# Mixture of experts: the slots of tokens counted in units of 128, with three positions of 128 slots among 32 of 256

## The chip, the cores and the metric

The kernel runs on one core of a Trainium2 chip. The metric is the time on the device in microseconds (us); the lower, the better. The engines of the core work side by side, each through its own list of instructions in order: TensorE (PE: matmuls and, as PEld, the loading of their stationary operand), VectorE (DVE), ScalarE (ACT), GpSimd (POOL) and SyncE (SP, which only issues transfers). Transfers run on 16 DMA engines that all queues share.

## The reference, cut to what matters

Two layers work on 4 images of 1024 tokens with 384 channels. Layer 0 is an attention and a mixture of experts, layer 1 an outlook attention and a feed-forward part. The change is in the experts of layer 0:

```python
scores = einsum('bsd,de->bse', x, gate_w) + gate_b          # 4 experts
probs = softmax(scores)
masked = probs * (probs among the token's two largest)
masked = masked / (sum(masked) + 1e-9)
h = gelu(einsum('bsd,edh->ebsh', x, w1) + b1, approximate=False)   # 384 -> 1536
y = einsum('ebsh,ehd->ebsd', h, w2) + b2                            # 1536 -> 384
out = einsum('bse,ebsd->bsd', masked, y)
```

Only two of the four experts have a weight other than zero for a token. There are 4096 tokens, so 8192 pairs of a token and an expert. How many tokens an expert gets depends on the data, so it is not known when the program is built.

## The kernel before, in words

Everything is float32. Attention runs first, then `experts`, then `rest` (the outlook attention in `outlook`, the feed-forward part in `Kron`).

**Slots and blocks.** Each token has two slots, one in the list of each of its experts. `Router.route` works out the slots of one image and writes for each slot a line of `table` in memory: the number of the token, its mean and its scale. An expert's list is cut into blocks of XB = 256 slots. As the last block of each of the 4 lists can be filled in part, the kernel is built for NXB = 35 blocks (8192 slots and 4 times 255, divided by 256). All 35 are always computed, whatever the data.

**The order of the blocks.** The first NFIRST = 4 blocks must be full with tokens of images 0 to 2, so that they can begin before the last image is routed; `Router.first` (L1369) picks them. `Router.schedule` (L1431) sets the order of the rest when the last image is routed. It counts for every image and expert how many blocks are begun, so that blocks come in the order in which the images complete them. It is VectorE work on arrays with a few numbers per partition. `Router.rows` (L1395) turns the counts into two lists of row numbers, one number per position: `w` for the rows of the weights of its expert, `t` for the rows of `table`. The last part of `schedule` works out `index`, the row of `yg` from which each token later fetches its two results. `schedule` is a generator: the block loop advances it by `next(beside)` once per up matmul group of blocks 0 to 2 (L1613), behind the last projections and the routing of the last image.

**One block** (`experts`, the loop from L1587). `tokens(n)` gathers the lines of the table, `fetch(n)` gathers the tokens into `xb`, one gather of 128 tokens for each of the block's two tiles, and `weights(n)` gathers the expert's weights, `up` (128 rows of 18,480 bytes) and `down` (128 rows of 19,968 bytes). These are indirect transfers of GpSimd. VectorE normalizes the tokens (`norm`), TensorE transposes them (`turn`) and VectorE copies the result into `xbT`. Then come twelve groups of three up matmuls (L1607: 128 rows, 128 columns of weights, 256 tokens), each with a gelu on ScalarE (L1611), and for each tile of 128 tokens twelve down matmuls (L1624, 384 columns). VectorE adds the bias (L1629) and SyncE writes the tile to `yg` in memory (L1630). Each float32 matmul shows as two records, here called passes.

**What is ahead of what.** The buffers `up`, `down`, `xb` and `xbT` exist twice, for even and odd blocks. At the start of block n the loads for block n+1 are issued in program order; `norm(n+1)` follows the up matmuls of block n, and `turn(n+1)` stands in TensorE's list before the last tile's down matmuls of block n. TensorE, VectorE, ScalarE and SyncE keep the order in which the program is written (a manual schedule); GpSimd's order is set by the framework when the program is built. In the outlook stage it is the other way round: SyncE and GpSimd keep the written order, the other three are ordered at build.

**Adding the results.** `add(i)` gathers a tile's two results from `yg`, weights them and adds them to the residual. Inside the experts one tile is added per block, as soon as all blocks that can hold the tokens of its image are done; `Router.complete(b)` (L1484) gives their number: 15, 23, 31 and 35 for images 0 to 3. That makes 19 tiles in the experts. The other 13 are added in the outlook stage, one in each of its steps from step 4 on (L1704).

Of the kernel before, what the change touches and what calls it, by code (L numbers as in the profile page):

```python
# [10 lines left out]
FP = mybir.dt.float32  # L11
# [32 lines left out]
XB = 256  # L44
NXB = (2 * NT * P + NE * (XB - 1)) // XB
NFIRST = 4


class Net:
# [16 lines left out]
    def slots(self, dram):  # L66

        self.table = dram.tile([NE * NT * P, Router.LINE], mybir.dt.int32, name="table")
        self.yg = dram.tile([NXB * XB, C], FP, name="yg")
        self.room = [dram.tile([P * (BAND + 1) * NH], FP, name=f"room_{t}", tag=f"room_{t}") for t in range(NB)]  # L70
# [1132 lines left out]


class Router:

# [9 lines left out]
    def __init__(self, net, pool, keep, psum):  # L1216
# [25 lines left out]
        self.number = const("number", [P, NXB])  # L1242
        count(self.number, [[1, NXB]])
        self.lane = const("lane", [P, 1])
# [3 lines left out]

        self.next = const("next", [P, B + 1, NE])
        nc.gpsimd.memset(self.next, 1.0)  # L1250
# [118 lines left out]
    def first(self):  # L1369

        nc = self.nc
        shape = [P, NE, self.NJ]
        full = self.temp("full", [P, NE])
        nc.vector.tensor_scalar(full, self.upto[:, B - 1, :], -float(XB), None, ALU.add)
        fills = self.temp("gt", shape)
        nc.vector.tensor_tensor(
            fills, full.unsqueeze(2).to_broadcast(shape), self.steps.unsqueeze(1).to_broadcast(shape), ALU.is_ge
        )
        nc.vector.tensor_reduce(full, fills, AX.X, ALU.add)

        self.start = self.pool.tile([P, B + 1, NE], FP, name="rt_start")
        self.begun = self.pool.tile([P, B + 1, NE], FP, name="rt_begun")
        nc.gpsimd.memset(self.begun[:, 0, :], 0.0)
        pre = self.start[:, 0, :]
        nc.gpsimd.memset(pre[:, 0:1], 0.0)
        for e in range(1, NE):
            nc.vector.tensor_tensor(pre[:, e : e + 1], pre[:, e - 1 : e], full[:, e - 1 : e], ALU.add)
        taken = self.begun[:, 1, :]
        nc.vector.tensor_scalar(taken, pre, -1.0, float(NFIRST), ALU.mult, ALU.add)
        nc.vector.tensor_scalar(taken, taken, 0.0, None, ALU.max)  # L1390
        nc.vector.tensor_tensor(taken, taken, full, ALU.min)
        nc.vector.tensor_scalar(pre, pre, float(NFIRST), None, ALU.min)
        self.firsts = self.rows(self.pool, "first", NFIRST, 1)

    def rows(self, pool, name, n, groups):  # L1395
# [6 lines left out]
        own = self.temp(f"own_{name}", [P, NE])  # L1402
        nc.vector.tensor_scalar(own, self.region, 1.0 / XB, None, ALU.mult)
        nc.vector.tensor_tensor(jump, jump, own.unsqueeze(1).to_broadcast([P, groups, NE]), ALU.add)
# [11 lines left out]
        for what, by, last in (  # L1416
            ("w", self.next[:, :groups, :].rearrange("p g e -> p (g e)"), None), ("t", step, NE * self.NJ - 1),
        ):
            nc.vector.tensor_tensor(part, past, by.unsqueeze(1).to_broadcast(shape), ALU.mult)
            row = self.temp(f"row_{what}_{name}", [P, n])  # L1420
            nc.vector.tensor_reduce(row, part, AX.X, ALU.add)
            if last is not None:
                nc.vector.tensor_tensor(row, row, self.number[:, :n], ALU.add)
                nc.vector.tensor_scalar(row, row, float(last), None, ALU.min)
            nc.vector.tensor_scalar(row, row, float(P), self.lane, ALU.mult, ALU.add)
            rows = self.pool.tile([P, n], mybir.dt.int32, name=f"rows_{what}_{name}")
            nc.vector.tensor_copy(rows, row)
            out.append(rows)
        return out

    def schedule(self, pool):  # L1431
# [3 lines left out]
        fills = self.temp("gt", shape)  # L1435
        taken = self.temp("taken", [P, NE])
        nc.vector.tensor_copy(taken, self.begun[:, 1, :])
        begun = self.temp("ends", [P, B + 1, NE])
        nc.vector.tensor_copy(begun[:, 0, :], taken)
        for b in range(B):  # L1440
            nc.vector.tensor_tensor(
                fills, self.upto[:, b + 1, :].unsqueeze(2).to_broadcast(shape),
                self.steps.unsqueeze(1).to_broadcast(shape), ALU.is_gt,
            )
            nc.vector.tensor_reduce(begun[:, b + 1, :], fills, AX.X, ALU.add)
            nc.vector.tensor_tensor(begun[:, b + 1, :], begun[:, b + 1, :], taken, ALU.max)

        nc.vector.tensor_copy(self.begun[:, 1:, :], begun[:, :B, :])
        fresh = self.temp("fresh", [P, B, NE])
        nc.vector.tensor_tensor(fresh, begun[:, 1:, :], begun[:, :B, :], ALU.subtract)  # L1450
        start = self.start[:, 1:, :]
        nc.vector.tensor_reduce(start[:, :, 0:1], begun[:, :B, :], AX.X, ALU.add)
        for e in range(1, NE):
            nc.vector.tensor_tensor(
                start[:, :, e : e + 1], start[:, :, e - 1 : e], fresh[:, :, e - 1 : e], ALU.add
            )
        yield
        self.all = self.rows(pool, "all", NXB, B + 1)
        yield

        groups = [P, B + 1, NE]
        wide = [P, NT, NE]
        region = self.region.unsqueeze(1).to_broadcast(groups)
        edge, base, move = (self.temp(n, groups) for n in ("edge", "bases", "move"))
        nc.vector.scalar_tensor_tensor(edge, self.begun, float(XB), region, ALU.mult, ALU.add)
        nc.vector.scalar_tensor_tensor(base, self.start, float(XB), edge, ALU.mult, ALU.subtract)
        nc.vector.tensor_copy(move[:, 0, :], base[:, 0, :])
        nc.vector.tensor_tensor(move[:, 1:, :], base[:, 1:, :], base[:, :B, :], ALU.subtract)
        row, past = self.wide(pool, "row", wide), self.wide(pool, "past", wide)
        nc.vector.tensor_tensor(row, self.at, move[:, 0:1, :].to_broadcast(wide), ALU.add)  # L1470
        for g in range(1, B + 1):
            nc.vector.tensor_tensor(past, self.at, edge[:, g : g + 1, :].to_broadcast(wide), ALU.is_ge)
# [10 lines left out]
    @staticmethod  # L1483
    def complete(b):  # L1484

        return min(NXB, NFIRST + (2 * NTOK * (b + 1) + NE * (XB - 1)) // XB)

    def gather(self, y, i, n):

        self.nc.gpsimd.indirect_dma_start(  # L1490
            out=y, out_offset=None, in_=self.net.yg[: self.complete(i // NB) * XB, :],
            in_offset=bass.IndirectOffsetOnAxis(ap=self.index[n][:, i : i + 1], axis=0),
        )


def experts(net, router, x1, x2, wup, wdown, beside):
# [10 lines left out]
    with ExitStack() as ctx:  # L1507
# [23 lines left out]
        ids, xbs = {}, {}  # L1531

        def tokens(n):
            t = ids[n] = halves[0].tile([P, TT, router.LINE], I32, name="ids", tag="ids", bufs=6)
            nc.gpsimd.indirect_dma_start(
                out=t.rearrange("p t w -> p (t w)"), out_offset=None,
                in_=net.table.rearrange("(r t) w -> r (t w)", t=TT),
                in_offset=bass.IndirectOffsetOnAxis(ap=rows(n)[1], axis=0),
            )

        def fetch(n):
            xb = xbs[n] = halves[n % 2].tile([P, TT, C], FP, name="xb", tag="xb")
            last = (B - 1 if n < NFIRST else B) * NTOK
            for t in range(TT):
                nc.gpsimd.indirect_dma_start(
# [4 lines left out]
        def norm(n):  # L1550
            xb = xbs[n]
            own = ids.pop(n).bitcast(FP)
            for t in range(TT):
                nc.vector.tensor_scalar(
# [3 lines left out]
        def turn(n):  # L1558
            xb = xbs.pop(n)
            xbT = halves[n % 2].tile([P, KC, XB], FP, name="xbT", tag="xbT")  # L1560
            for t in range(TT):
                ps = router.psum()
# [24 lines left out]
        for n in range(NXB):  # L1587
# [13 lines left out]
            up, down = ws.pop(n)  # L1601
            hs = []
            for f in range(NF):
                ps = ps_h.tile([P, XB], FP, name="ps_h", tag="h")
                for k in range(KC):
                    o = k * HID + f * P
                    nc.tensor.matmul(  # L1607
                        ps, lhsT=up[:, o : o + P], rhs=xbT[:, k, :], start=k == 0, stop=k == KC - 1,
                    )
                h = hp.tile([P, XB], FP, name="h", tag="h")  # L1610
                nc.scalar.activation(h, ps, AF.Gelu, bias=up[:, KC * HID + f : KC * HID + f + 1])  # L1611
# [5 lines left out]
            else:  # L1617
                net.scale(0, added)
            for t in range(TT):
                if t == TT - 1 and n + 1 < NXB:  # L1620
                    xbT = turn(n + 1)
                ps = ps_y.tile([P, C], FP, name="ps_y", tag="y")
                for f in range(NF):
# [6 lines left out]
                nc.sync.dma_start(  # L1630
                    out=net.yg[n * XB : (n + 1) * XB, :].rearrange("(p t) c -> p t c", t=TT)[:, t, :], in_=y
                )
# [606 lines left out]
```

## Time and profile before

| | |
|---|---|
| median of 3 runs | 2905.45 us (2903.23 to 2907.56) |
| the profiled execution | 2905.3 us, of which its span is 2903.6 |
| mean granted clock of TensorE | 0.965 |
| attention, to the first up matmul of the experts | 0 to 1210.6 us |
| experts, blocks 0 to 34 | 1210.6 to 2345.5 us |
| rest | 2345.5 to 2903.6 us |

The page's second part cuts the span into 40 slices and gives the busy share of each engine in tenths:

```
PE   6889998999999987799999999999999999999988
DVE  1377776777778786532010001111111146877642
ACT  3778777787778774212112111211211122122135
POOL 1000000120021004122111122212121101100000
PEclk9989999999999998799999999999999999999998
DMA  5143435222413334445545455555555437644432
```

Slices 17 to 31 are the experts. How to read such lines: in rows of groups, the columns are line, engine, operation, output and inputs by the program's names, shapes and count, then busy time in us and the mean in ns of one, then the engine's idle time before them and what ended it. In rows in order of time the columns are start and duration in us, engine, line, operation, names, shape and count, and in brackets the idle time before and what released the instruction.

### The profile page before, as it was taken

The page shows a single profiled execution, that of the slowest core. Times are in us where ns is not written, and L with a number is a line of the kernel's source. Part 1 is how long each engine was busy: PE and PEld are TensorE (multiplying, and loading weights), DVE is VectorE, ACT ScalarE, POOL GpSimd, SP SyncE. Part 2 cuts the span into 40 slices and gives each one's busy share as a digit, 9 for nine tenths or more (in the row PEclk, how much of TensorE's full clock was granted, in tenths as well). Part 3 has the DMA queues.
Part 4 walks back from the last instruction along what each step waited for, and adds up shares of the span by engine and source line. Part 5 has one row for each costly group of instructions (what it writes and reads, how often), then busy time and mean ns, then how long its engine had stood idle before and what let it go on. Part 6 is the DMA issues. An engine that isn't in the chain of part 4 may idle for free. (4 is left out here: it accounts for less than half of the span.)

```text
span 2903.6 us, 37519 instructions
## 1 busy us (share of the span) xinstructions
PE 2715.6 (94%) x13632; PEld 1453.0 (50%) x13632; DVE 1347.6 (46%) x3714; ACT 1208.3 (42%) x2023; POOL 401.3 (14%) x500
## 2 busy tenths in 40 slices
PE   6889998999999987799999999999999999999988
PEld 3323333333333322367777777777777754444432
DVE  1377776777778786532010001111111146877642
ACT  3778777787778774212112111211211122122135
POOL 1000000120021004122111122212121101100000
PEclk9989999999999998799999999999999999999998
DMA  5143435222413334445545455555555437644432
GB/s 104 32 103 100 100 92 140 66 59 70 109 44 75 80 90 128 130 149 201 190 169 195 168 200 204 200 212 201 214 202 204 162 132 222 193 161 155 145 106 89
DMA packets 216996, 405.97 MB, mean 140 GB/s; under 512 B 83505, under 2 KB 177905, under 8 KB 203745
## 3 DMA queue, kind: packets, MB, share of 16 engines
q1 hardware_dynamic: 185504, 189.20, 22.2%
q0 software_dynamic: 27152, 209.66, 21.1%
q10 hardware_dynamic: 4144, 4.61, 0.5%
q8 instruction: 110, 1.80, 0.3%
q14 instruction: 86, 0.70, 0.1%
HBM read 305.35 MB, written 49.99 MB: 122 GB/s over the span
## 5 line engine op out<-in xcount | busy, mean ns | idle before, releaser
L1611 ACT ACTIVATE h<-ps_h,up 128x256 f32<-128x256 f32 x420 | 199.0, 474 | 916.5 <-PE ps_h L1607 916.4
L1607 PE MATMUL ps_h<-xbT,up 128*128 128x256 f32 x2520 | 553.5, 380 | 2.6 <-ACT h L1611 1.8
L1624 PE MATMUL ps_y<-down,h 128*128 128x384 f32 x1680 | 554.5, 487 | 0.0
L1607 PEld LDWEIGHTS ps_h<-xbT,up 128*128 128x128 f32 x2520 | 479.9, 191 | 77.9 <-ACT h L1611 2.7
L685 DVE CUSTOM_DVE_ANT_0 e<-e,rz,inv 128x1024 f32<-128x1024 f32 x384 | 475.2, 1274 | 51.8 <-DMA rz<-r_row 49.2
L633 ACT ACTIVATE e<-ps_s,ten 128x1024 f32<-128x1024 f32 x384 | 408.1, 1109 | 59.8 <-PE ps_s L623 36.2
L1624 PEld LDWEIGHTS ps_y<-down,h 128*128 128x128 f32 x1680 | 317.3, 191 | 207.0 <-issue 1.2
L1629 DVE TENSOR_TENSOR y<-ps_y,down 128x384 f32<-128x384 f32 x70 | 39.0, 557 | 718.1 <-PE ps_y L1624 718.1
L623 PE MATMUL ps_s<-q,k 32*128 32x512 f32 x1536 | 295.5, 667 | 53.4 <-ACT e L633 31.5
L641 PE MATMUL ps_o<-e,wv 128*32 128x512 f32 x1536 | 226.1, 664 | 40.5 <-DVE wv L692 39.0
L641 PE MATMUL ps_z<-e,rt_ones 128*32 128x512 f32 x1536 | 218.6, 643 | 0.0
L712 POOL DMA_DIRECT2D q<-po x96 | 76.1, 878 | 946.4 <-DMA q<-po 514.6
L369 ACT ACTIVATE below<-tk_left,tk_bound 128x1024 bf16<-128x1024 f32 (+1 forms) x160 | 184.3, 1152 | 52.3 <-DVE tk_bound L375 42.1
L623 PEld LDWEIGHTS ps_s<-q,k 32*128 32x128 f32 x1536 | 92.0, 189 | 192.2 <-ACT e L633 92.0
L1735 PE MATMUL ps_a<-wa,xnT 128*128 128x486 f32 x384 | 167.6, 585 | 8.7 <-DVE attn L1745 7.0
L284 PE MATMUL ps_t<-xnT,wqkv 128*128 128x512 f32 x288 | 137.1, 617 | 2.4 <-ACT xnT L466 1.7
L641 PEld LDWEIGHTS ps_o<-e,wv 128*32 128x32 f32 x1536 | 31.5, 111 | 199.7 <-issue 68.4
L1735 PEld LDWEIGHTS ps_a<-wa,xnT 128*128 128x128 f32 x384 | 71.7, 192 | 93.4 <-issue 85.3
L641 PEld LDWEIGHTS ps_z<-e,rt_ones 128*32 128x32 f32 x1536 | 52.3, 117 | 132.0 <-issue 128.7
L1576 DVE SCALAR_TENSOR_TENSOR x<-yt,weight,x 128x384 f32<-128x384 f32 x38 | 23.5, 619 | 188.3 <-DMA x<-x 187.6
L1837 PE MATMUL ps_y<-band,v 128*32 128x194 f32 (+2 forms) x960 | 102.7, 517 | 8.0 <-DMA band<-room 7.7
L1490 POOL DMA_INDIRECT yt<-yg,index x64 | 65.5, 1024 | 305.9 <-DVE x L1576 142.4
(346 smaller groups left out, 2739.5 us busy)
## 6 DMA issues: line engine op xcount, KB each, us to landing
band<-room SPq DMA_DIRECT2D x32, 1560.0 KB
rz<-r_row SPq DMA_DIRECT2D x48, 512.0 KB
yg<-y SPq DMA_DIRECT2D x70, 192.0 KB
q<-q SPq DMA_DIRECT2D x192, 64.0 KB
k<-k SPq DMA_DIRECT2D x192, 64.0 KB
room<-none SPq DMA_DIRECT2D x64, 192.0 KB
x<-x SPq DMA_DIRECT2D x38, 192.0 KB
o<-in_x_dram SPq DMA_DIRECT2D x33, 192.0 KB
```

The source lines that it names most:

```text
L284: nc.tensor.matmul(ps, lhsT=lhsT(k), rhs=rhs(k), start=k == 0, stop=k == KC - 1)
L369: nc.scalar.activation(junk[:n], left[:n], AF.Sign, bias=bound[:n], accum_out=over[:n])
L623: nc.tensor.matmul(ps[:, half * 512 : half * 512 + 512], lhsT=self.k4[r, u * P : (u + 1) * P], rhs=self.q4[r, :], start=True, stop=True,)
L633: nc.scalar.activation(e, ps, AF.Exp, bias=shift, scale=QK_SCALE)
L641: nc.tensor.matmul(ps[r : r + 32, :], lhsT=lhsT(odd), rhs=self.es[2 * u + odd][:, half * 512 : half * 512 + 512], start=u == 0, stop=u == ...
L685: nc.vector.tensor_tensor_reduce(self.es[m], self.es[m], self.rz, 1.0, self.im["inv"][:, m, self.h : self.h + 1], ALU.mult, ALU.add, self. ...
L712: nc.gpsimd.dma_start(out=there, in_=po[r : r + 32, :], accum_op=ALU.add)
L1607: nc.tensor.matmul(ps, lhsT=up[:, o : o + P], rhs=xbT[:, k, :], start=k == 0, stop=k == KC - 1,)
L1611: nc.scalar.activation(h, ps, AF.Gelu, bias=up[:, KC * HID + f : KC * HID + f + 1])
L1624: nc.tensor.matmul(ps, lhsT=hs[f][:, t * P : (t + 1) * P], rhs=down[:, f * C : (f + 1) * C], start=f == 0, stop=f == NF - 1,)
L1735: nc.tensor.matmul(pa[:, hh, :HW_], lhsT=xnT[:, k, :], rhs=wa[:, k, hh * HW_ : (hh + 1) * HW_], start=k == 0, stop=k == KC - 1,)
L1837: nc.tensor.matmul(ys[c][32 * n : 32 * n + 32, lo - 512 * half : hi - 512 * half], lhsT=vs[b, t][:, h * HD : (h + 1) * HD], rhs=bands[b, t ...
```

## The change

Slots are counted in units of 128. There are NFULL = 32 positions of 256 slots and NHALF = 3 of 128. The order of positions is: four full ones (0 to 3, as before), three of 128 slots (4 to 6), and 28 full ones (7 to 34). `schedule` gives the three short positions to experts whose remaining slots end in the first half of a block of 256; if more than 32 full blocks would otherwise be needed, it gives one to the first 128 slots of such a block. `first_row(n)` is the row of `yg` at which position n begins.

```diff
-NXB = (2 * NT * P + NE * (XB - 1)) // XB
+NFULL = 2 * NT * P // XB
+NHALF = NE - 1
+NXB = NFULL + NHALF
 NFIRST = 4
+NLEAD = NFIRST + NHALF
+UNITS = XB // P
...
+def first_row(n):
+
+    half = min(max(n - NFIRST, 0), NHALF)
+    return (n - half) * XB + half * P
```

`first` scales its two results by UNITS (one more instruction). `rows` works on B + 2 = 6 groups of 4 experts in place of 5, and scales the rows in up to three pieces:

```diff
-            nc.vector.tensor_scalar(row, row, float(P), self.lane, ALU.mult, ALU.add)
+            for first, end in ((0, min(n, NFIRST)), (NFIRST, min(n, NLEAD)), (NLEAD, n)):
+                if first < end:
+                    size = P if last is None or first == NFIRST else P // UNITS
+                    own = row[:, first:end]
+                    nc.vector.tensor_scalar(own, own, float(size), self.lane, ALU.mult, ALU.add)
```

In `schedule` the choice of the short positions comes first, then the counts per image:

```diff
+        part, left, odd, pairs, sums = (self.temp(n, [P, NE]) for n in ("base", "part", "share", "run", "prob"))
+        nc.vector.tensor_scalar(part, self.upto[:, B, :], -float(P), None, ALU.add)
+        blocks(pairs, part)
+        blocks(odd, self.upto[:, B, :])
+        nc.vector.tensor_tensor(odd, odd, pairs, ALU.subtract)
+        ahead(sums, odd)
+        nc.vector.tensor_scalar(sums, sums, NHALF + 0.5, None, ALU.is_lt)
+        nc.vector.tensor_tensor(odd, odd, sums, ALU.mult)
+        nc.vector.scalar_tensor_tensor(left, first, -1.0 / UNITS, pairs, ALU.mult, ALU.add)
+        nc.vector.tensor_scalar(left, left, 0.5, None, ALU.is_gt)
+        ahead(sums, left)
+        nc.vector.tensor_scalar(sums, sums, 1.5, float(UNITS), ALU.is_lt, ALU.mult)
+        nc.vector.tensor_tensor(left, left, sums, ALU.mult)
+        ahead(sums, pairs)
+        nc.vector.tensor_scalar(sums, sums, NFULL + 0.5, None, ALU.is_gt)
+        nc.vector.scalar_tensor_tensor(odd, left, sums[:, NE - 1 :], odd, ALU.mult, ALU.add)
+        nc.vector.tensor_tensor(taken, first, odd, ALU.add)
+        yield
+
+        ends = self.temp("ends", [P, B, NE])
+        for b in range(B):
+            nc.vector.scalar_tensor_tensor(part, taken, -float(P), self.upto[:, b + 1, :], ALU.mult, ALU.add)
+            blocks(ends[:, b, :], part)
...
+        nc.gpsimd.memset(start[:, 1, 0:1], float(UNITS * NFIRST))
+        nc.gpsimd.memset(start[:, 2, 0:1], float(UNITS * NFIRST + NHALF))
...
-        for g in range(1, B + 1):
+        for g in range(1, B + 2):
             nc.vector.tensor_tensor(past, self.at, edge[:, g : g + 1, :].to_broadcast(wide), ALU.is_ge)
             nc.vector.tensor_tensor(past, past, move[:, g : g + 1, :].to_broadcast(wide), ALU.mult)
             nc.vector.tensor_tensor(row, row, past, ALU.add)
```

Here `blocks` is a comparison of 64 elements and a sum, and `ahead` a copy and three additions of single columns, each on the one before. What depends on the number of positions follows:

```diff
-        return min(NXB, NFIRST + (2 * NTOK * (b + 1) + NE * (XB - 1)) // XB)
+        return min(NXB, NLEAD + (2 * NTOK * (b + 1) + NHALF * (XB - 1)) // XB)
```

`complete` then gives 17, 25, 33 and 35. In `experts` every loop over the two tiles of a block runs over `tiles(n)`, and the matmuls of a short position have 128 tokens:

```diff
+        def tiles(n):
+            return 1 if NFIRST <= n < NLEAD else TT
...
-            for t in range(TT):
+            for t in range(tiles(n)):
                 nc.gpsimd.indirect_dma_start(
                     out=xb[:, t, :], out_offset=None, in_=x1[:last, :],
...
+            size = tiles(n) * P
             for f in range(NF):
-                ps = ps_h.tile([P, XB], FP, name="ps_h", tag="h")
+                ps = ps_h.tile([P, XB], FP, name="ps_h", tag="h")[:, :size]
...
-                        ps, lhsT=up[:, o : o + P], rhs=xbT[:, k, :], start=k == 0, stop=k == KC - 1,
+                        ps, lhsT=up[:, o : o + P], rhs=xbT[:, k, :size], start=k == 0, stop=k == KC - 1,
...
-            for t in range(TT):
-                if t == TT - 1 and n + 1 < NXB:
+            for t in range(tiles(n)):
+                if t == tiles(n) - 1 and n + 1 < NXB:
                     xbT = turn(n + 1)
```

## The prediction, made before the kernel was run

> **What bounds the kernel now.** I read three views in this order: the page's busy shares, then the order of work on TensorE inside one expert block, then VectorE and GpSimd in the stretch where the schedule is worked out.
>
> ```profile
> PE 2715.6 (94%) x13632; PEld 1453.0 (50%) x13632; DVE 1347.6 (46%) x3714; ACT 1208.3 (42%) x2023; POOL 401.3 (14%) x500
> ...
> L1607 PE MATMUL ps_h<-xbT,up 128*128 128x256 f32 x2520 | 553.5, 380 | 2.6 <-ACT h L1611 1.8
> L1624 PE MATMUL ps_y<-down,h 128*128 128x384 f32 x1680 | 554.5, 487 | 0.0
> ```
>
> TensorE is busy 94% of the span, and the two expert matmuls stand for 1108 us of it with 2.6 us of idle time before them. Inside a block (start, duration, line, count):
>
> ```profile
> 1332.35 15.70 PE L1607 MATMUL ps_h<-xbT,up 128*128 128x256 f32 x72
> 1347.89 7.90 PE L1624 MATMUL ps_y<-down,h 128*128 128x384 f32 x24
> 1355.63 0.82 PE L1564 MATMUL ps_t<-ident,xb 128*128 128x128 f32 x6
> 1356.29 7.91 PE L1624 MATMUL ps_y<-down,h 128*128 128x384 f32 x24
> 1364.03 15.70 PE L1607 MATMUL ps_h<-xbT,up 128*128 128x256 f32 x72
> ```
>
> No row has a wait. From start to start: 15.54 us for 72 passes of the up matmul (0.216 us each, an fp32 matmul being two records), 7.74 us for the 24 passes of one tile of the down matmul (0.3225 each), 0.65 us for six transposes, 7.74 us again: 31.68 us a block, 35 times. In the expert stage time is TensorE's passes and nothing else. So what counts is how many passes go, what a pass costs at 128 columns, and whether a shorter block still finds its weights, tokens and schedule ready.
>
> **Passes removed.** Before: 35 blocks of 256 slots. After: 35 positions still, 32 of 256 and 3 of 128 (numbers 4, 5 and 6). A position of 128 keeps its 72 up passes, over 128 columns in place of 256, has 24 down passes in place of 48, and three transposes in place of six. The down part is certain: 24 x 0.3225 = 7.74 us; the transposes give 3 x 0.109 = 0.33 us. The up pass at 128 columns with two-pass fp32 weights is in no row. The two rows nearest to it are these:
>
> ```profile
> 2374.31 0.47 PE L1800 MATMUL ps_c<-u,shift 128*128 128x180 f32 x2
> 2374.61 0.47 PE L1800 MATMUL ps_c<-u,shift_-1_15514 128*128 128x180 f32 x2
> ...
> 1280.13 0.36 PE L1326 MATMUL ps_t<-rt_run,rt_before 128*128 128x4 f32 x2 [0.19 <-DVE rt_run L1320]
> 1280.35 0.36 PE L1327 MATMUL ps_t<-rt_run,rt_ones 128*128 128x4 f32 x2
> ```
>
> At 180 columns two passes take 0.30 us, 0.152 each, which is 180 x 0.84 ns, the slope of the 256- and 384-column rows: the weight load, though its record is 188 ns long, is hidden. At 4 columns two passes take 0.22 us, 0.11 each: that is the pace of loading weights. At 128 columns the columns need 128 x 0.84 = 0.108 us, so both limits meet at 0.11. A rule speaks against taking that: the Trainium skill, "TensorE: Matmul & The Clock Gate", section "Back-to-back issue gap", says the spacing in a stream of loads and matmuls is set by both operations, and gives 81 ns at 128 columns where the isolated gap is 56, a factor of 1.45. By the rule a pass would be some 0.156 us (my estimate, from that factor), by the rows 0.11. The rows are this kernel's own fp32 passes, so I take 0.11; if the load were not hidden at all, 0.108 + 0.11 = 0.22 and the up part would gain nothing. Up part: 72 x (0.216 - 0.110) = 7.6 us. One short position saves 7.6 + 7.74 + 0.33 = 15.7 us and lasts 16.0; three save **47.1 us** (37 by the rule, 24 with no overlap).
>
> **Can the short positions be fed?** Every position still gathers its whole weights, 128 rows of 18,480 and 19,968 bytes, 4.9 MB. Their rows:
>
> ```profile
> 1348.90 0.94 POOL L1524 DMA_INDIRECT up<-in_wup_dram,rows_w_all  x1 [13.33 <-ACT h L1611]
> 1356.73 0.94 POOL L1545 DMA_INDIRECT xb<-x,ids  x1 [6.89 <-PE ps_t L1564]
> 1357.98 0.95 POOL L1545 DMA_INDIRECT xb<-x,ids  x1 [0.30 <-issue]
> 1365.06 0.94 POOL L1524 DMA_INDIRECT down<-in_wdown_dram,rows_w_all  x1 [6.14 <-DVE y L1629]
> ```
>
> The load of "up" is released when the gelus of the block before last end, and is needed a whole block after the one now running: issued some 48 us ahead of its use, landing in 9.2 us (10.1 for "down"). Laid end to end that is 19.3 us a position against a short position's 16.0, so the loads of three short positions pile up. Serving them one after another, from the end of position 3's up part, I get "up" of position 7 landing some 9 us before it is needed, the tightest of all; in the 2 us windows of the load the DMA ran at 425 to 449 GB/s, so the bytes alone need only 11 us. Hence nothing. Bounds: 0 to 6 us a position if landings took 22 us and the lead were gone. The gelu record takes 0.474 us at 256 columns and one is due every 0.66 us: hidden too. Token and yg transfers get fewer.
>
> **What the schedule adds.** It runs on VectorE under block 2, and behind it in program order stands norm(3), which TensorE's transposes for block 3 need:
>
> ```profile
> 1301.35 0.17 DVE L1437 COPY rt_taken<-rt_begun 128x4 f32<-128x4 f32 x1
> ...
> 1305.66 0.88 DVE L1410 TENSOR_TENSOR rt_past_all<-rt_number,rt_start 128x700 f32<-128x700 f32 x1
> ...
> 1318.29 0.86 DVE L1554 TENSOR_SCALAR xb<-xb,ids 128x384 f32<-128x384 f32 x2
> ...
> 1323.96 0.82 PE L1564 MATMUL ps_t<-ident,xb 128*128 128x128 f32 x6
> ```
>
> Norm(3) is done at 1319.15, needed at 1323.96: 4.8 us of cover. The first part goes from 20 VectorE instructions in 3.65 us to 49 by my count. Most of the 29 new ones hang on the one before and are 4 wide, 0.17 us long and 0.2 apart: 29 x 0.19 = 5.5 us. In rows(), five wide instructions grow from 700 to 840 elements (0.88 to about 1.03 us: +0.75) and two scalings become three each (+0.6). One more group in the move loop: 0.98 us. Together 7.8 us, so norm(3) starts at 1326.1. After block 0, where TensorE also waited for a norm, its transposes started 0.6 us after the norm did and the next matmul 1.05 after that; here that gives 1327.75 in place of 1324.61: a stall of **3.1 us**, once. With instructions 0.08 apart it would be under 1 us, with 0.25 about 5. Behind norm(3) on VectorE stand only block 2's y and the copies of turn(3), which nobody needs for 7.7 us. The clock can add to it: the idle time of 3.93 us at 1247.7 was followed by a clock of 0.58 in 1252 to 1256, and 24 down passes that elsewhere take 7.90 us took 9.23 (+1.3). The same page of the skill, section "What's actually happening", has the clock fall after an idle window of about 3.4 us that runs freely. I put the idle time itself at 2.6 us, so by the rule no halving, and none in the sum; 1.3 us stays in the range. GpSimd gets two small memsets, ready long before; GpSimd lets such work slip ahead (it issued xb of block 3 at 1253, before its weights), so nothing, at most 1 us. The weight rows come 6 us later, at about 1315, and the loads of position 4 some 7 us later than 1321; they land near 1338 and are needed at 1367.
>
> **Adds moved.** complete() gives 17, 25, 33 in place of 15, 23, 31, so 17 tiles are added inside the experts and 15 in the outlook stage, in place of 19 and 13. Inside the experts an add hides under TensorE. In the outlook VectorE waits for the gathers, 15.1 us in nine waits between 2385 and 2500, and TensorE idles 12 us in that stretch. From 2495 on, where the two new adds come, TensorE idles 0.8 us in 155 with VectorE 74% busy; an add is about 1.9 us of VectorE (two of 0.61, 0.55, 0.17). I take **1 us** (0 to 5: this stage's order is made anew at build).
>
> **Sum** against the profiled execution's own 2905.3 us (span 2903.6): 2905.3 - 47.1 + 3.1 + 1.0 = 2862.3. The median of the runs is 2905.45, so the forecast is 2862.5.
>
> **Rivals.**
> A. The weight load shows at 128 columns: for it the skill's rule, against it the 180-column row. A pass between 0.156 and 0.22: 2872.5 to 2886.
> B. The short positions are bound by DMA: for it 19.3 us of landings against 16.0, against it the lead of a whole block. At 19.3 to 22 us each, 10 to 18 us come back: 2872 to 2881.
> C. The other side. GpSimd's fixed order is made anew for uneven blocks. If the load of "up" came to stand behind the xb gather of the block that is running (released 24 us into it), it would land 24 + 1.3 + 9.2 = 34.5 us in, 2.8 us after the block's end; over 31 positions that is 87 us, about 2949. It decides from 1.5 us a position. Against it: today's order follows the releases, and a shorter block moves them all together.
> That the count of positions stays 35 is no rival: the passes fall whatever slots are filled.
>
> **Chances.** Forecast 0.70, A 0.12, B 0.08, C 0.05, and 0.05 for something that I don't see, shared out alike. The first three are all faster. The range 2856 (no stall, no cost of adds) to 2880 holds the forecast and most of A and B, and leaves C out. No change means within 0.2%, 5.8 us: 0.02. Slower: C and a share of the unseen, 0.07. Faster: 0.91.
>
> **What would show it.** Up passes over 128 columns 0.11 us apart, 72 of them in about 7.9 us, x216 in all, with down passes x1608; short positions starting 16 us apart with no DMA wait; transposes of block 3 about 3 us late behind norm(3); the outlook stage as long as before within 5 us. Up passes at 0.15 or more would make the forecast wrong by A, waits for up or down at positions 5 to 7 by B, such waits at every position by C.

## The result and the profile after

The changed kernel takes 2856.91 us, median of four runs (2853.06 to 2861.66), beside 2905.39 us for four runs of the kernel before: a ratio of 0.9834, 95% interval 0.9816 to 0.9851. The profiled execution takes 2858.5 us with a span of 2856.8, 46.8 us shorter than the span of before. The forecast was 2862.5, within 2856 to 2880.

The page after, its first part and the two groups of expert matmuls:

```profile
PE 2668.3 (93%) x13551; PEld 1423.0 (50%) x13551; DVE 1349.2 (47%) x3742; ACT 1202.5 (42%) x2023; POOL 398.0 (14%) x501
...
L1661 PE MATMUL ps_h<-xbT,up 128*128 128x256 f32 (+1 forms) x2520 | 531.5, 371 | 2.5 <-ACT h L1665 1.8
L1678 PE MATMUL ps_y<-down,h 128*128 128x384 f32 x1608 | 530.3, 487 | 0.0
```

The count of up passes is unchanged (2520, 216 of them in a second shape), the down passes are 72 fewer, and TensorE's busy time falls by 47.3 us. The idle sums before these two groups hardly move, so the shorter work was not given back as waits for weights. The order of work on TensorE (start, duration, line, shape, count, and in brackets the idle time before it) shows where that holds and where it doesn't:

```profile
1308.46 7.90 PE L1678 MATMUL ps_y<-down,h 128*128 128x384 f32 x24
1319.30 1.51 PE L1617 MATMUL ps_t<-ident,xb 128*128 128x128 f32 x6 [2.94 <-DVE xb L1607]
1320.61 8.72 PE L1678 MATMUL ps_y<-down,h 128*128 128x384 f32 x24
1329.16 15.70 PE L1661 MATMUL ps_h<-xbT,up 128*128 128x256 f32 x72
...
1360.51 8.20 PE L1661 MATMUL ps_h<-xbT,up 128*128 128x128 f32 x72
1368.55 0.49 PE L1617 MATMUL ps_t<-ident,xb 128*128 128x128 f32 x3
1368.88 7.91 PE L1678 MATMUL ps_y<-down,h 128*128 128x384 f32 x24
1376.62 8.20 PE L1661 MATMUL ps_h<-xbT,up 128*128 128x128 f32 x72
```

The lower half is the first short position: 8.04 us from the start of its up matmuls to its transposes, 0.33, 7.74, and the next begins 16.11 us after it, without a bracket. The upper half is the end of block 2: the transposes for block 3 wait 2.94 us for norm(3).

Cut by stage, with the starts of TensorE's rows as the cuts and the end of the last expert matmul as the last one (us):

| stage | before | after | difference |
|---|---|---|---|
| start to the first up matmul of the experts | 1210.56 | 1208.10 | -2.5 |
| block 0, up part | 29.26 | 29.78 | +0.5 |
| block 0, down part | 21.95 | 16.14 | **-5.8** |
| block 2, down part | 16.14 | 20.70 | **+4.6** |
| block 3 | 31.68 | 31.35 | -0.3 |
| positions 4 to 6 | 95.04 | 48.65 | **-46.4** |
| positions 7 to 34 | 886.46 | 886.47 | 0.0 |
| from the end of the experts | 558.1 | 561.2 | +3.1 |

Block 1 and the up part of block 2 are left out; they last the same in both (38.9 and 15.5 us). Three rows carry the result. Two were in the forecast (positions 4 to 6, block 2). The third, block 0's down part, was not, and its instructions are the same ones in both kernels.

In block 2, VectorE's row of the first part of the schedule, one of its wide instructions, and norm(3):

```profile
1293.60 0.16 DVE L1468 TENSOR_SCALAR rt_base<-rt_upto 128x4 f32<-128x4 f32 x1
...
1303.76 1.02 DVE L1423 TENSOR_TENSOR rt_past_all<-rt_number,rt_start 128x840 f32<-128x840 f32 x1
...
1318.69 0.86 DVE L1607 TENSOR_SCALAR xb<-xb,ids 128x384 f32<-128x384 f32 x2
```

From the schedule's first instruction to norm(3) it is 25.09 us, and it was 16.94 before: 8.15 us more. The idle time is short, but the clock falls behind it. In this view of stretches the columns are: stretch and length, busy time and count of PE, PEld, DVE, ACT and POOL, then the granted clock, the DMA share and GB/s:

```profile
1316.30:1319.30 3.00, 0.07 (x1) 0.03 (x1) 2.76 (x11) 0.00 (x0) 2.39 (x3) 0.92 0.98 419
1319.30:1322.00 2.70, 2.70 (x9) 2.09 (x10) 1.83 (x4) 0.00 (x0) 1.62 (x2) 0.50 0.78 301
1322.00:1325.00 3.00, 3.00 (x11) 1.78 (x10) 0.00 (x0) 0.00 (x0) 0.94 (x1) 0.96 0.12 26
1325.00:1329.00 4.00, 4.00 (x14) 2.41 (x13) 0.00 (x0) 0.00 (x0) 0.00 (x0) 1.00 0.09 34
```

Right behind the wait TensorE runs at half its clock for some 2.9 us. The mean of 0.92 over the 3 us before shows that the fall came inside the wait, about 0.5 us before its end; shorter stretches of the same view put the halved time at 1318.8 to 1322.2, 3.4 us. That is why the six transposes take 1.51 us in place of 0.82 and the 24 down passes 8.72 in place of 7.90, and why a wait of 2.94 us lengthens the block by 4.6.

Block 0 is read from three engines. First before. On TensorE the transposes wait for norm(1). On VectorE norm(1) stands behind the addition of a residue, `o`, which waits for its load:

```profile
1251.65 1.26 PE L1564 MATMUL ps_t<-ident,xb 128*128 128x128 f32 x6 [3.93 <-DVE xb L1554]
1252.70 9.23 PE L1624 MATMUL ps_y<-down,h 128*128 128x384 f32 x24
```

```profile
1249.77 0.56 DVE L756 TENSOR_TENSOR o<-o,ps_t 128x384 f32<-128x384 f32 x1 [9.39 <-DMA o<-in_x_dram]
1251.05 0.84 DVE L1554 TENSOR_SCALAR xb<-xb,ids 128x384 f32<-128x384 f32 x2
```

That load (192 KB, SyncE's queue) was issued at 1240.88, 4.0 us after the store of an earlier tile, `x<-o`. GpSimd had issued the gather of block 2's "up" (2.4 MB) 2.1 us before the load:

```profile
1236.88 0.39 SPq L761 DMA_DIRECT2D x<-o  x1
1240.88 0.33 SPq L738 DMA_DIRECT2D o<-in_x_dram  x1
```

```profile
1238.81 0.94 POOL L1524 DMA_INDIRECT up<-in_wup_dram,rows_w_first  x1 [19.32 <-ACT h L1611]
```

After, the same three engines (TensorE; VectorE; SyncE and GpSimd):

```profile
1237.88 7.90 PE L1678 MATMUL ps_y<-down,h 128*128 128x384 f32 x24
1245.62 0.82 PE L1617 MATMUL ps_t<-ident,xb 128*128 128x128 f32 x6
```

```profile
1239.28 0.56 DVE L760 TENSOR_TENSOR o<-o,ps_t 128x384 f32<-128x384 f32 x1 [1.48 <-DMA o<-in_x_dram]
1240.56 0.84 DVE L1607 TENSOR_SCALAR xb<-xb,ids 128x384 f32<-128x384 f32 x2
```

```profile
1234.19 0.38 SPq L765 DMA_DIRECT2D x<-o  x1
1236.85 0.33 SPq L742 DMA_DIRECT2D o<-in_x_dram  x1
```

```profile
1236.87 0.94 POOL L1574 DMA_INDIRECT up<-in_wup_dram,rows_w_first  x1 [19.85 <-ACT h L1665]
```

Here the load is issued 0.02 us ahead of the gather. Its addition starts 2.4 us after the issue; before, it started 8.9 us after it. Counted from the first up matmul of the experts, the load went out at +30.3 before and at +28.8 after, the gather at +28.3 and +28.8.

What held the load is that store. `o` has two buffers, so the load of the sixth tile needs the buffer from which the fourth is stored; SyncE's waits from 1209 to 1242 of before name it (us in all, times, longest):

```profile
SPq L738 <- DMA x<-o: 10.8, 3, 5.2
```

The load went out 4.0 us after the store was issued before, 2.7 us after it in the changed kernel.

### The profile page after: what moved, and what is told of

Its sections match the earlier page's. It is cut to its first block, busy times and chain, and to the rows that moved or that the text cites. A ratio compares the mean times of both kernels' runs of the same rounds, so it can differ in the third digit from the quotient of the medians.

```text
span 2856.8 us, 37367 instructions
## 1 busy us (share of the span) xinstructions
PE 2668.3 (93%) x13551; PEld 1423.0 (50%) x13551; DVE 1349.2 (47%) x3742; ACT 1202.5 (42%) x2023; POOL 398.0 (14%) x501
## 5 line engine op out<-in xcount | busy, mean ns | idle before, releaser
L1665 ACT ACTIVATE h<-ps_h,up 128x256 f32<-128x256 f32 (+1 forms) x420 | 194.7, 464 | 873.3 <-PE ps_h L1661 872.7
L1661 PE MATMUL ps_h<-xbT,up 128*128 128x256 f32 (+1 forms) x2520 | 531.5, 371 | 2.5 <-ACT h L1665 1.8
L1678 PE MATMUL ps_y<-down,h 128*128 128x384 f32 x1608 | 530.3, 487 | 0.0
L1661 PEld LDWEIGHTS ps_h<-xbT,up 128*128 128x128 f32 x2520 | 463.9, 191 | 72.5 <-ACT h L1665 2.7
L1678 PEld LDWEIGHTS ps_y<-down,h 128*128 128x128 f32 x1608 | 303.6, 191 | 197.6 <-issue 0.8
L645 PE MATMUL ps_o<-e,wv 128*32 128x512 f32 x1536 | 227.8, 668 | 48.4 <-DVE wv L696 46.8
L645 PEld LDWEIGHTS ps_z<-e,rt_ones 128*32 128x32 f32 x1536 | 52.4, 118 | 131.7 <-issue 127.9
```

What stands on the lines that cost most here:

```text
L645: nc.tensor.matmul(ps[r : r + 32, :], lhsT=lhsT(odd), rhs=self.es[2 * u + odd][:, half * 512 : half * 512 + 512], start=u == 0, stop=u == ...
L1661: nc.tensor.matmul(ps, lhsT=up[:, o : o + P], rhs=xbT[:, k, :size], start=k == 0, stop=k == KC - 1,)
L1678: nc.tensor.matmul(ps, lhsT=hs[f][:, t * P : (t + 1) * P], rhs=down[:, f * C : (f + 1) * C], start=f == 0, stop=f == NF - 1,)
```

## The experiments

Theory, at this point: the short positions give 46.7 us, the schedule costs 4.6 through norm(3), and 5.8 us come from a race in block 0 between the residue load and the weight gather, which the change wins by accident or by something upstream. Rivals: block 0 differs from execution to execution with no connection to the change; the two more tiles that are added in the outlook cost part of the 3.1 us at the end; a longer chain of short positions would run out of weights.

The runs were made on four chips; on three of them the kernel before takes 2945 to 2952 us, so each is compared with the kernel before on its own chip.

**Both kernels once more**, unchanged, and again later.

> The kernel before, unchanged, for a second profile. In its first profile TensorE waited 3.9 us between the two down tiles of block 0 (norm(1) behind the load of a residue tile), and 21.95 us went from the first of these tiles to block 1 in place of 16.14. If that wait belongs to the kernel before, it stands here again, 4 to 6 us long in all. If it is a race between that load and a gather of weights which goes one way or the other in each execution, it can be gone, with a time some 5 us shorter.

> The changed kernel, unchanged, for a second profile. Short positions again 16.1 us apart and the wait for norm(3) again about 2.9 us, as both are set by instructions. The wait for norm(1) between the down tiles of block 0, absent in the first profile, is absent again if the change took it away, and can appear (4 to 6 us) if it is a race.

> The changed kernel, unchanged, timed beside the others on one chip. Expected 46 to 49 us below the kernel before on a chip like that of the first measurement (0.984), more where the wait for norm(3) has cover from other waits of block 2. Its block 0 is expected without the wait for norm(1), as in its two profiles so far.

> The changed kernel, unchanged, on the same chip as the two others. Block 0 without the wait for norm(1) a fourth time if its early residue loads are a property of the program; with it, if it was chance. The gain of the change against the kernel before with the residue loads ahead is expected 5.8 us smaller than against the kernel before: that part of the 48.5 us was not the short positions.

The kernel before took 2945.1 us, the changed one 2883.7, in one run each; the repeats below give the size of the gain. The stall in block 0 came again in the kernel before (TensorE, then VectorE) and not in the changed one, where its down part took 16.14 us:

```profile
1278.39 1.47 PE L1564 MATMUL ps_t<-ident,xb 128*128 128x128 f32 x6 [4.41 <-DVE xb L1554]
```

```profile
1276.51 0.55 DVE L756 TENSOR_TENSOR o<-o,ps_t 128x384 f32<-128x384 f32 x1 [9.20 <-DMA o<-in_x_dram]
```

Short positions took 16.11 us again. The timed repeats: a_timed 2897.1 us beside 2951.5 (0.9820, 0.9803 to 0.9837), a_third 2894.2 beside 2945.7 (0.9821, 0.9804 to 0.9838). So on these chips the gain is 51.5 to 54.4 us. What is missing there is the stall of norm(3): in the up part of block 2 ScalarE comes 6 us late, for a reason that the trace calls "remote", and TensorE waits for it (ScalarE; TensorE; of a_third):

```profile
1344.05 1.20 ACT L1665 ACTIVATE h<-ps_h,up 128x256 f32<-128x256 f32 x3 [24.98 <-remote]
```

```profile
1344.58 14.75 PE L1661 MATMUL ps_h<-xbT,up 128*128 128x256 f32 x54 [6.06 <-ACT h L1665]
```

In these 6 us VectorE goes on with the schedule, and norm(3) is in time. So the wait of 2.9 us that was expected of a_again did not come. Without the 4.6 us of the first profile the sum of its stages would be -51.4, near what these chips show.

**norm(3) earlier** in the changed kernel: ahead of the up matmuls of block 2, so ahead of the schedule on VectorE; and, in a second kernel, norm(1) to norm(3) all so.

```diff
+            early = n == NFIRST - 2
+            if early:
+                norm(n + 1)
...
-            if n + 1 < NXB:
+            if early:
+                pass
+            elif n + 1 < NXB:
                 norm(n + 1)
```

> The changed kernel with norm(3) put ahead of the schedule in VectorE's order, nothing else. If the schedule costs time only by what stands behind it, the wait of 2.9 us and the halved clock after it go, together 4.6 us: about 2852 us against 2857 for the changed kernel, and down tiles of block 2 in 16.1 us in place of 20.7. If the later rows of the schedule also hold up the loads of position 4, waits for up or xb appear there instead and the time stays near 2857.

> The changed kernel with norm(1), norm(2) and norm(3) put at the head of blocks 0, 1 and 2 in VectorE's order, ahead of the residue adds, the routing and the schedule. If the schedule costs time by what stands behind it alone, the wait for norm(3) goes: down tiles of block 2 in 16.1 us (20.7 in the first profile of the changed kernel), and 4.6 us less than the changed kernel where that wait shows. Nothing is expected from norm(1), which did not wait in the changed kernel. If the schedule's later rows are what holds block 3 or 4, the time stays.

With norm(3) alone: 2891.1 us, ratio 0.9808 (0.9790 to 0.9825). With `early = n < NFIRST - 1`: 2897.3, ratio 0.9835 (0.9812 to 0.9858), no gain over the unchanged kernel on the same chip. The first tells nothing about the stall, as ScalarE covered it here with or without the edit; on a chip where norm(3) is waited for it was not tried. In the second a projection waits 4.0 us in block 0 for a VectorE instruction (`gate_o`) that now stands behind norm(1), which itself waits 20.1 us for its tokens, and block 0 takes 52.4 us in place of 45.6 to 46.5.

**The same in the kernel before**: norm(1) to norm(3) early.

```diff
+            early = n < NFIRST - 1
+            if early:
+                norm(n + 1)
```

> The kernel before with norm(1), norm(2) and norm(3) at the head of blocks 0, 1 and 2; all 35 blocks at 256 slots. If the wait of 4 us and the slow clock after it in block 0 are a wait for norm(1) behind the residue load, they go: 16.1 us from the first down tile of block 0 to block 1 in place of 21.9 to 22.4, and 5.8 us less than the kernel before. Then 5.8 us of the gain of the change were not the short positions. If TensorE waits there for something else (the gather of xb, say), nothing changes.

2948.03 us, ratio 0.9990 (0.9977 to 1.0003). The down part of block 0 has no wait left (16.14 us), yet block 0 lasts 51.8 us: a new wait has come in its up part. At the head of VectorE's list norm(1) waits for its own tokens, the residue additions stand behind it, and a projection of the last image waits for one of them (VectorE; TensorE).

```profile
1265.75 0.89 DVE L1554 TENSOR_SCALAR xb<-xb,ids 128x384 f32<-128x384 f32 x2 [20.90 <-DMA xb<-x,ids]
```

```profile
1267.32 3.69 PE L284 MATMUL ps_t<-wproj,q 128*128 128x388 f32 x6 [4.14 <-DVE gate_o L757]
```

The first of these additions starts 21.7 us after the first up matmul (13.2 before), the gather of block 2's "up" goes out at +34.7, behind the sixth load (+32.1), and no residue waits for its load. So this edit took one wait away and made another, and the 5.8 us expected from it did not come. It cannot tell whether the load or norm(1) itself set the stall of block 0; the rows of before speak for the load.

**The load itself earlier**, in the kernel before: five buffers for `o`, and the loads issued three tiles ahead instead of one, so that the sixth goes out long before the gather.

```diff
-                o = late[0].tile([P, C], FP, name="o", tag="o", bufs=2)
+                o = late[0].tile([P, C], FP, name="o", tag="o", bufs=5)
...
-            if t + 1 < NB:
-                residue(B - 1, t + 1)
+            for u in range(1, 4) if t == 0 else (t + 3,):
+                if u < NB:
+                    residue(B - 1, u)
```

> The kernel before with the residue tiles of the last image in five buffers in place of two and their loads issued three tiles ahead; all else as before. If the 5.8 us in block 0 are the sixth residue load meeting the gather of block 2's weights, no residue load comes after that gather any more: 16.1 us from the first down tile of block 0 to block 1, and about 5.8 us less than the kernel before. If it is something else, 21.9 to 22.4 us stay there.

The stall is gone and has not moved elsewhere: block 0 lasts 45.8 us.

```profile
1275.47 7.90 PE L1625 MATMUL ps_y<-down,h 128*128 128x384 f32 x24
1283.21 0.82 PE L1565 MATMUL ps_t<-ident,xb 128*128 128x128 f32 x6
1283.86 7.91 PE L1625 MATMUL ps_y<-down,h 128*128 128x384 f32 x24
1291.61 1.46 PE L1608 MATMUL ps_h<-xbT,up 128*128 128x256 f32 x6
```

The experts take 1139.9 us by the profile, beside 1146.2 and 1146.0 of the two kernels with the stall (b_again, b_lateadds). The whole time is 2942.73, ratio 0.9991 (0.9974 to 1.0007): a difference of 3 us whose interval holds both 0 and the 6 that the stage shows. The cause is shown by the stage; the time doesn't resolve it. The five buffers also free the loads from the wait for a store, so the edit does not tell whether the gather meets the load alone or already the store ahead of it.

**The same edit in the changed kernel**, together with norm(3) early.

> The changed kernel with the residue loads ahead as in the run beside it, and norm(3) ahead of the schedule. Its block 0 had no wait before, so the loads bring it nothing there. On a chip where norm(3) waits, 4.6 us less than the changed kernel; where another wait of block 2 covers it, 0 to 1.5 us less. Down tiles of block 2 in 16.1 us either way.

2897.2 us, ratio 0.9824 (0.9807 to 0.9842), beside 2894.2 of the unchanged one: nothing to win, since on this chip neither stall was there. The pair b_ahead and a_ahead3 gives nearly the passes alone, as neither has a stall: 1139.9 - 1092.7 = 47.2 us in the experts, of which 46.7 lie in blocks 3 to 6 and 0.5 in small differences ahead of them.

**The adds alone**, in the kernel before: `complete` gives two positions more, so that 17 tiles are added in the experts and 15 in the outlook, as after the change.

```diff
-        return min(NXB, NFIRST + (2 * NTOK * (b + 1) + NE * (XB - 1)) // XB)
+        return min(NXB, NFIRST + 2 + (2 * NTOK * (b + 1) + NE * (XB - 1)) // XB)
```

> The kernel before with complete() two higher, so that 17 tiles are added in the experts and 15 in the outlook stage, as in the changed kernel; all 35 blocks stay at 256 slots. The prediction put the moved adds at 1 us (0 to 5): 2906.4. The first profiles have the stage after the experts 3.1 us longer: 2908.5. If those 3.1 us are only the clock and the order of that execution, no difference within 2 us.

2946.07 us beside 2949.55, ratio 0.9986 (0.9973 to 0.9999): no cost. From the first transposes of the outlook to the end of the span, the profiles with 15 adds there take 552.4 to 559.8 us (nine of them, among these after, 559.8, and a_norm3, 552.4) and those with 13 take 553.7 to 560.9 (five of them, before 556.7). The 3.1 us at the end of the first pair lie inside that scatter.

**Thirteen short positions** in place of three, to see whether the weights keep up. It is the kernel before with one tile in positions 4 to 16; half of their slots are left out and their results stand twice in `yg`.

```diff
+        def tiles(n):
+            return 1 if NFIRST <= n < NFIRST + 13 else TT
...
-            for t in range(TT):
+            for t in range(tiles(n)):
...
+            size = tiles(n) * P
...
-                        ps, lhsT=up[:, o : o + P], rhs=xbT[:, k, :], start=k == 0, stop=k == KC - 1,
+                        ps, lhsT=up[:, o : o + P], rhs=xbT[:, k, :size], start=k == 0, stop=k == KC - 1,
```

> The kernel before with 13 positions (4 to 16) cut to their first 128 slots, and each of their results written to two rows; half of the slots of these positions are left out, so the output is not the reference's. It asks whether weights of 4.9 MB can be had every 16 us in a long row. By the bytes (425 to 449 GB/s in the load windows, 11 us a position) every short position lasts 16.1 us and the kernel is 13 x 15.6 = 203 us faster. By the landings end to end (9.2 + 10.1 us) the lead of a block is used up after some four positions, and the later ones last 19.3 us: about 170 us faster, with waits for up or down.

Twelve of them stand 16.11 us apart, with no wait for "up" or "down"; the last takes 25.58. The time was 2749.5 us in its one run, 202 less than the median of the kernel before on its chip, as expected for positions of 16.1 us (203).

```profile
1565.08 8.20 PE L1611 MATMUL ps_h<-xbT,up 128*128 128x128 f32 x72
...
1581.18 8.20 PE L1611 MATMUL ps_h<-xbT,up 128*128 128x128 f32 x72
...
1597.29 8.20 PE L1611 MATMUL ps_h<-xbT,up 128*128 128x128 f32 x72
...
1612.15 1.51 PE L1567 MATMUL ps_t<-ident,xb 128*128 128x128 f32 x6 [6.67 <-DVE xb L1557]
```

```profile
1609.54 1.27 DVE L1579 SCALAR_TENSOR_TENSOR x<-yt,weight,x 128x384 f32<-128x384 f32 x2 [11.49 <-DMA x<-x]
```

Over 200 us of this chain (the columns as above) TensorE has no gap, while the DMA engines are busy nine tenths of the time:

```profile
1400.00:1600.00 200.00, 200.00 (x1226) 160.12 (x1225) 18.61 (x37) 53.72 (x147) 48.11 (x51) 1.00 0.89 335
```

So 4.9 MB per 16.1 us can be had, with little to spare. The first thing to break is not a weight but a small load: the first add's `x` (192 KB) was issued at 1598.92, 0.6 us behind a gather of "down" (1598.32), its addition started 10.6 us after that, VectorE was idle for 11.5 us, and norm(17) stands behind it. This looks like block 0 a second time; no edit tried it here. The run also shows block 0 without the stall (45.3 us), though its code up to block 3 is that of the kernel before.

**The last part of the schedule twice**, in the changed kernel: the row loop and the two index lists repeated.

```diff
+        for _ in range(2):
             nc.vector.tensor_tensor(row, self.at, move[:, 0:1, :].to_broadcast(wide), ALU.add)
             for g in range(1, B + 2):
```

> The changed kernel with the last part of the schedule (the rows of each token and the two index lists) worked out twice, some 7.3 us more of VectorE work ahead of norm(3), nothing else. On a chip where another wait of block 2 covers norm(3) in the changed kernel, 1.4 us of cover are left (profile a_third), so TensorE waits about 5.9 us for it ahead of the transposes for block 3, and the clock may be halved for some 3.4 us after that: 6 to 8 us more. On a chip like that of the first profile, 10 to 12 us from the first down tile of block 2 on top of 16.1. If the schedule is hidden in another way, the down tiles of block 2 still take 16.1 to 20.7 us.

It ran on a chip where the kernel before takes 2905.8 us and norm(3) is waited for. The way from the schedule's first instruction to norm(3) is 7.2 us longer, and so is the wait:

```profile
1309.82 7.90 PE L1679 MATMUL ps_y<-down,h 128*128 128x384 f32 x24
1327.87 1.51 PE L1618 MATMUL ps_t<-ident,xb 128*128 128x128 f32 x6 [10.15 <-DVE xb L1608]
1329.18 8.65 PE L1679 MATMUL ps_y<-down,h 128*128 128x384 f32 x24
1337.66 15.70 PE L1662 MATMUL ps_h<-xbT,up 128*128 128x256 f32 x72
```

10.15 us in place of 2.94, block 2's down part 27.84 in place of 20.70, positions 4 to 6 still 16.1 each, the time 2865.5 us, ratio 0.9861 (0.9834 to 0.9888). In this stage each further microsecond on VectorE was one on TensorE, and it went by norm(3) alone. The loads of the short positions don't feel it.

## Why the prediction was right, point by point

- **Passes removed**, -47.1: measured -46.7 (positions 4 to 6 -46.4, block 3's transposes -0.3), and 47.2 between the two kernels without stalls. An up pass at 128 columns came to 8.04 / 72 = 0.1117 us where the sum had 0.110. The reading of the two rows held, though 0.108 by the columns and 0.11 by the loads lie too close together to tell which of them sets the pace; the 0.156 worked out from the skill's rule (same page as below, "Back-to-back issue gap") was not seen in these fp32 streams. Rival A falls.
- **Feeding**, 0: right, in three positions and in twelve on end. Rivals B and C fall: no position from 7 on is longer (886.47 beside 886.46). One step of it was not as forecast: the "up" of position 4, expected some 7 us later, went out 19.5 us after the first up matmul of block 2, where it was 20.5 before. The rows of the weights did come 6.6 us later, but GpSimd's order was made anew and sent this load ahead of most of the token lists. (The lead of "up", given as 48 us, is 46.8: 1348.90 to 1395.71, the start of block 5.)
- **The schedule**, VectorE +7.8: measured +8.15. Wait 2.6: measured 2.94. Stall 3.1: measured 4.6. The term that was mis-sized is the clock: of the difference about 0.4 us are the longer wait and 1.1 the transposes and passes at half clock. The sum left it out, as the wait would be shorter than the idle window of about 3.4 us that the Trainium skill names ("TensorE: Matmul & The Clock Gate", "What's actually happening"), and kept 1.3 us for it in the range. (A little of it was in the sum unseen: in the yardstick from block 0 the six transposes took 1.26 us in place of 0.82.) Here the clock stood at half for 3.4 us, the length of that window, but it fell about 2.5 us after the last matmul. The measurement decides: a wait shorter than that window is not safe from it.
- **Adds**, +1: not to be told from 0. Alone they gave a ratio of 0.9986.
- **Block 0**, not in the sum: -5.8. The prediction used the stall there as the yardstick for norm(3), and never asked what ended it: one row further up, on VectorE, was a wait of 9.39 us for a load. That was the step left out. Scatter came on top: -2.5 before the experts, whose work there is that of before, and +3.1 behind them. Against the forecast's -43.0 the terms went off by +0.4 (passes), +1.5 (stall), +2.1 (behind the experts, 3.1 for 1.0), -2.5, +0.5 (block 0, up part) and -5.8, together -3.8: the -46.8 of the profile. The forecast was near the median because most of its terms were, and because the rest in part cancelled: +4.5 against -8.3. The largest single error is a term that it didn't have. That 2856.91 still lies in the range, 0.9 us above an end drawn for no stall at all, is luck in part.

How the race turned out went with the short positions: three profiles of kernels with 35 full blocks and the original order of loads and norms have the stall (before, b_again, b_lateadds), with the load issued 2 to 2.6 us after the gather; seven with short positions (after, a_again, a_norm3, a_timed, a_third, a_twice, b_short13) have not, with the load at +28.3 to +28.9 from the first up matmul and the gather at +28.1 to +29.4. In all ten the load waits for the store of the fourth tile. It goes out 3.9 to 4.1 us after that store in the three, where the gather begins 1.4 to 1.9 us after the store, and 2.5 to 2.7 us after it in the seven, where the gather begins 2.2 to 3.3 us after it. So it seems that the gather first delays the store, and then the load that waited for it; this is read from ten profiles, and no edit moved the store alone. Upstream, the third residue's addition starts at +22.5 to +23.1 in the former and +21.9 to +22.4 in the latter. Why it comes some 0.7 us earlier on the mean with short positions is **open**: b_short13 has the same code up to block 3 and the same buffers in memory as the kernel before. So the 5.8 us are shown to be the residue load going out behind the gather, and are not shown to belong to the change. Without them the change is worth 46.7 - 4.6 = 42.1 us where norm(3) is waited for.

## What to carry to other kernels

Where TensorE is the bound and a stage shows no waits, count passes and price each by the nearest rows of the same data type and stream: at 128 columns these cost about half of what they cost at 256 (0.1117 and 0.216 us), with a weight load at each. A wait in the profile of before that the change doesn't touch belongs in the range with both signs: follow it back to the transfer that ends it, and see how near its issue stands to a large gather's. And a small load that an in-order engine needs should be issued well ahead of the large ones, or all that stands behind it on that engine waits too. Look also at what frees its buffer: with two buffers here that was the landing of a store.

## What the hardware showed that was not expected

- A change of order by 2 us is worth 6: a load of 192 KB was followed by its addition 2.4 us after issue when it went out level with a gather of 2.4 MB, and 8.9 us after issue when it went out 2.1 us behind it.
- TensorE's clock fell to 0.50 about 2.5 us into an idle time of 2.94 us and stood there 3.4 us (1318.8 to 1322.2). In block 0 of the kernel before it fell 4.2 us after the last matmul, 0.3 us into the next work, and again stood there 3.4 us (1252.0 to 1255.4); in a_twice it fell 2.7 us into the idle time and stood there 10.2 us. No fixed idle time sets it off in these three. Behind the 10.15 us of a_twice the same 24 passes took no longer than behind 2.94 (8.65 us beside 8.72), as the idle time itself took up most of the slow stretch.
- On three chips the kernel before is 40 to 46 us slower, and the first gelu of ScalarE in block 2 comes so late that TensorE waits 6 us for it; what holds it is in no row, and it stays open.
